# Layer 1 of a convolution-attention hybrid: the norm rows' parts for the experts behind the next image's keys and values

## The chip, the cores and the metric

The kernel runs on one core of one Trainium2 chip, in one launch. The metric is the time of the whole kernel on the device, in microseconds (us). The engines are named as the profile names them: PE is TensorE (matmuls; PEld is its weight load), DVE is VectorE, ACT is ScalarE, POOL is GpSimd, SP is the engine that issues the DMAs here.

## The reference

Eight images of 256 channels and 32 x 32 points pass through two layers. Layer 0 is convolutional attention and a filtered feed-forward network. Layer 1, in which the change lies, treats each image as 1024 tokens of 256 numbers:

```python
t = _to_tokens(x)
t = t + _L1_attn_ref(_ln_t(t), L1_attn_WQ, L1_attn_WK, L1_attn_WV)
t = t + _L1_ffn_ref(_ln_t(t), L1_ffn_Wr, ..., L1_ffn_bo)
x = _from_tokens(t, x)
```

The attention is causal, with one head: scores of queries and keys, the lower triangle kept, exponentials divided by their sum, times the values. The feed-forward part has eight experts of three matrices each, and a gate that is computed from the mean over the images of the second norm's rows:

```python
feat = jnp.mean(x, axis=0)
w = jax.nn.softmax(feat @ Wr + br, axis=-1)
h = jnp.einsum('bfd,edh->bfeh', x, W1) + b1
...
y = jnp.einsum('bfeh,ehd->bfed', h, Wo) + bo
return jnp.einsum('bfed,fe->bfd', y, w)
```

## The kernel before, in words

Layer 0 ends at about 1387 us of the profiled execution, layer 1's attention runs from there to about 1957 us, and the experts from there to the end.

**The attention of layer 1.** One image is one turn of a loop, `together(causal(b), beside(b), 0.85)`. `causal(b)` is the main part: for each of eight blocks of 128 queries, the scores (`s`, two halves of 512 keys), the negated row maximum (`nm`), the exponential (`pr`), mask and sum (`norm`), the turning of the rows (`tp`, copied to `pT`) and, for each pair of blocks, the product with the values (`po`, added to `t`). The stages of a block follow with a lag, so the last products of image b stand among the first scores of image b + 1. `beside(b)` is the work that other images need:

- `first_norm(b + 1)`: the first norm of the next image. The tokens are turned (`tpt`, copied to `zt`), VectorE takes their statistics (`st`, `mv`), GpSimd works out the scale in eight small operations (`y`, `r`), ScalarE scales, TensorE turns back (`tpz`), ScalarE copies to `z`.
- `second_norm(b - 1)`: the same for the image before, into `z2` (the profile calls the turned rows of both norms `z`), after its attention is done. Then `u_d` is stored, the image after next but one is loaded, GpSimd adds the rows to `feat` (line 1583), and `z_parts` splits them.
- `z_parts` (line 1589): the experts multiply in a split precision. For each half of 512 tokens ScalarE writes a rounded upper part, VectorE subtracts it (`parts`) and forms a combination of the two in place (`z`), and two DMAs store the three parts in `z_d`, from where the expert stage fetches them.
- `keys_values_of(b + 1)`: the next image's keys `kk` (four steps `pk` of TensorE, each copied by ScalarE) and values `v` (four steps `pv`, likewise).
- `chore(n)`: n steps of `expert_parts` (line 1500), which splits one expert weight matrix after another (`we`, `parts_w`, four VectorE operations each), until they are used up in image 6.

The scores of image b + 1 need `kk` and `v` of that image, so all of `beside(b)` is emitted before image b + 1 begins. `together` interleaves by estimated times that the generators yield:

```python
for us in main:
    a += us
    while side is not None and s < ratio * a:
        step = next(side, None)
        ...
for _ in side or ():
    pass
```

What is left of the side when the main part ends is emitted without a main step between. The side's estimates are 1.7 for each step of keys or values, 4.8 for each half in `z_parts` and 1.0 for a chore.

**Order on the engines.** Instructions of `pe`, `dve`, `act` and `pool` go through `InOrder`: each is kept behind the instruction that was emitted before it on its engine, so that one that waits holds up all behind it. DMAs on `nc.sync`, and the few instructions that are issued on `nc.vector` or `nc.scalar` directly, may be placed elsewhere by the planner.

**Memory.** PSUM banks for `pk`, `pv`, `po` and half of the norms' turns come from one pool with two buffers (tag `mm`), those for `tp` and the other half of the norms' turns from another with two (tag `tp`), the scores from a third with two. `z2` has one buffer, `parts` two, `we` and `parts_w` one each.

Of the kernel before, what the change touches and what calls it, by code (L numbers as in the profile page):

```python
# [105 lines left out]
def conv_attn_hybrid_kernel(  # L106
# [424 lines left out]
    def keys_values(zb, kk, v, at, wv_s, bank):  # L531
        for h in range(2):
            hs = slice(h * HALF, (h + 1) * HALF)
            for g in range(KC):
                pk = bank([P, HALF], "pk")
                for k in range(KC):
                    pe.matmul(pk, at[:, k, g * P : (g + 1) * P], zb[:, k, hs], start=(k == 0), stop=(k == KC - 1))
                act.copy(kk[:, g, hs], pk)
                yield 1.7
        for j in range(0, NT, 2):  # L540
            pv = bank([P, 2, C], "pv")
            for i in range(2):
                js = slice((j + i) * P, (j + i + 1) * P)
                for k in range(KC):
                    pe.matmul(pv[:, i, :], zb[:, k, js], wv_s[:, k, :], start=(k == 0), stop=(k == KC - 1))
            act.copy(v[:, j : j + 2, :], pv)
            yield 1.7
# [828 lines left out]
    def tokens(stack, early, early_stack):  # L1376
# [55 lines left out]
        def gate(h, room, bank):  # L1432

            nt = NT // 2
            lg = bank([P, nt, NE], "lg")
            for i in range(nt):
                c0 = i * P
                for k in range(KC):
                    pe.matmul(lg[:, i, :], feats[h][:, k, c0 : c0 + P], wrs[:, k, :], start=(k == 0), stop=False)
                pe.matmul(lg[:, i, :], ones[0:1, :], brs, start=False, stop=True)  # L1440
            yield 2.0
            ge = room([P, nt, NE], "ge", 1)
            gs = room([P, nt], "gs", 1)
            dve.tensor_reduce(gs, lg, AX.X, ALU.max)
            dve.tensor_sub(ge, lg, gs.unsqueeze(2).to_broadcast([P, nt, NE]))
            act.activation(ge, ge, AF.Exp)
            yield 1.0
            dve.tensor_reduce(gs, ge, AX.X, ALU.add)
            dve.reciprocal(gs, gs)
            dve.tensor_mul(ge, ge, gs.unsqueeze(2).to_broadcast([P, nt, NE]))  # L1450
            ge4 = room([P, nt, 4, NE], "ge4", 1)
            stacked(ge4, ge, (0, 1, 0, 1))
            yield 1.0
            pwT = bank([4 * NE, HALF], "pwT")
            for i in range(nt):
                pe.transpose(pwT[:, i * P : (i + 1) * P], ge4[:, i].rearrange("p a e -> p (a e)"), ident)
            dve.tensor_copy(wT[:, h * HALF : (h + 1) * HALF], pwT)
            yield 0.5
# [3 lines left out]
        with ExitStack() as l1:  # L1462
# [13 lines left out]
            def load_t(b):  # L1476
                t[b] = early["t"][b % 3] if b % 3 < 2 else two.tile([P, KC, N], F32, tag="t", name="t1", bufs=1)
                nc.sync.dma_start(t[b], t_d[b])
# [59 lines left out]
            zs = {}  # L1538
            chores = expert_parts()

            kk_of, v_of = {}, {}

            def room(shape, tag, bufs):
                return tiny.tile(shape, F32, tag=tag, name=tag, bufs=bufs)
# [9 lines left out]
            def ring(b, name, shape):  # L1554
                return early[name] if b % 2 == 0 else two.tile(shape, F32, tag=name, name=name, bufs=1)

            def first_norm(b):
                z[b] = ring(b, "z", [P, KC, N])
                yield from layer_norm(t[b], z[b], early["zt"], room, bank)

            def keys_values_of(b):
                kk_of[b], v_of[b] = ring(b, "kk", [P, KC, N]), ring(b, "v", [P, NT, C])
                yield from keys_values(z[b], kk_of[b], v_of[b], early["at"], early["wv"], bank_kv)
# [4 lines left out]
            def until(what):  # L1568
                while what not in done:
                    yield 0.7  # L1570

            def second_norm(b):
                yield from until((b, N // QC - 1))
                z2 = two.tile([P, KC, N], F32, tag="z2", name="z2", bufs=1)
                yield from layer_norm(t[b], z2, early["zt"], room, bank)
                nc.sync.dma_start(u_d[b], t[b])
                if b + 3 < B:
                    load_t(b + 3)
                for h, feat in enumerate(feats):
                    half = z2[:, :, h * HALF : (h + 1) * HALF]  # L1580
                    if b == 0:
                        pool.tensor_copy(feat, half)
                    else:
                        pool.tensor_add(feat, feat, half)
                for h in range(2):
                    yield from z_parts(b, h, z2[:, :, h * HALF : (h + 1) * HALF])

            def z_parts(b, h, src):
                parts = two.tile([P, 2, KC, HALF], F32, tag="parts", name="parts")
                act.activation(parts[:, 0].bitcast(F32R), src, AF.Copy, scale=DOWN)  # L1590
                yield 1.2
                dve.tensor_sub(parts[:, 1], src, parts[:, 0])
                yield 1.2
                dve.scalar_tensor_tensor(src, parts[:, 1], -STEP, parts[:, 0], ALU.mult, ALU.add)
                yield 2.4
                nc.sync.dma_start(z_d[b][:, h, :2], parts)
                nc.sync.dma_start(z_d[b][:, h, 2], src)

            def last_norm():

                for qc in range(HALF // QC, N // QC):
                    yield from until((B - 1, qc))
                yield from layer_norm(t[B - 1][:, :, HALF:], z2_last, early["zt"], room, bank)
                dve.tensor_add(feats[1], feats[1], z2_last)
                nc.sync.dma_start(u_d[B - 1][:, :, HALF:], t[B - 1][:, :, HALF:])
                yield 0.5
# [79 lines left out]
            def beside(b):  # L1686

                def chore(n):
                    for _ in range(n):
                        next(chores, None)  # L1690
                        yield 1.0

                if b + 1 < B:
                    yield from first_norm(b + 1)
                yield from chore(3)
                if b >= 1:
                    yield from second_norm(b - 1)
                yield from chore(2)
                if b + 1 < B:
                    yield from keys_values_of(b + 1)  # L1700
                else:
                    yield from last_norm()
                    yield from gate(1, room, bank)
                yield from chore(2)
# [13 lines left out]
            for b in range(B):  # L1718
                together(last() if b == B - 1 else causal(b), beside(b), 0.85)
# [5 lines left out]
        with ExitStack() as l2:  # L1725
# [176 lines left out]
            for n in range(len(pieces) + LAG3):  # L1902
                one_ = two_ = three = iter(())
                if n < len(pieces):
                    v, s = pieces[n]
                    G, h, b = visits[v]
# [34 lines left out]
    with ExitStack() as stack:  # L1941
        tokens(stack, early, early_stack)

    with tc.If(nc.values_load(bad[0:1, 0:1]) > 0):
        layer0_shifted()
        with ExitStack() as stack:
            tokens(stack, None, ExitStack())
# [112 lines left out]
```

## Time and profile before

| | us |
|---|---|
| runs | 3103.87, 3097.66, 3103.89 |
| median | 3103.87 |
| profiled execution | 3097.64 |
| its span | 3095.9 |
| PE busy | 2921.8 (94%) |
| DVE busy | 2340.2 (76%) |
| ACT busy | 1621.0 (52%) |
| POOL busy | 316.6 (10%) |

The span runs from the first to the last instruction of the profiled execution, and the durations in this text are from that execution. The images of the attention begin at 1510.7, 1583.5, 1656.3, 1729.1 and 1802 us (images 2 to 6), the last one at 1876 us.

In the lines of the profile, a row of the timeline has its start in us, the time taken in us, the engine, the line (L73 is the line in `InOrder` by which nearly all instructions are issued, so that they are told apart by their tiles), the operation, output and inputs by the program's names, the shapes, the count of merged instructions, and in brackets the idle time before it and what ended that. A row of the waits has the total in us, how often, and the longest. Tiles with `_e` are the other buffer of the same data (`z` and `z_e`, `kk` and `kk_e`), `te` and `t` are images.

### The profile page before, as it was taken

Reading aid. Unit: us, or ns where it says so; the run is one execution under the profiler, and the core shown is the slowest. Engines: PE = TensorE matmul, PEld = TensorE weight load, DVE = VectorE, ACT = ScalarE, POOL = GpSimd, SP = SyncE. Lnnn points to the kernel's source line nnn. Section 1 sums busy time; section 2 is a strip of 40 time slices with the busy share of each in tenths; the row PEclk is TensorE's granted clock in tenths of the full one; section 3 lists DMA queues with packets and bytes.
Section 4 is the critical chain, followed back from the end, with each engine's and each line's share of the span. In section 5 each row is a group of like instructions: output and inputs, shape, how many; then the busy total and the mean of one; then the engine's idle time right before and its main releaser. Section 6 shows DMA issues by size and latency. Waiting matters only on the chain.

```text
span 3095.9 us, 41592 instructions
## 1 busy us (share of the span) xinstructions
PE 2921.8 (94%) x16802; PEld 1928.7 (62%) x16802; DVE 2340.2 (76%) x2886; ACT 1621.0 (52%) x2440; POOL 316.6 (10%) x453
## 2 busy tenths in 40 slices
PE   6988899989998989889999999999999999999998
PEld 4644555555555555456666666677777777777776
DVE  2378787878787879686666655588988888888887
ACT  2555454545454545434444443565666666666664
POOL 1012111111111110001222222000000000000000
PEclk8999999999999999999999999999999999999999
DMA  6202121121213120103332311421211252112210
GB/s 194 53 5 66 44 60 51 50 60 47 64 38 73 36 61 15 36 23 116 143 131 109 123 65 81 164 72 66 102 68 68 71 201 75 68 68 95 76 68 29
DMA packets 63856, 234.87 MB, mean 76 GB/s; under 512 B 5590, under 2 KB 13862, under 8 KB 54822
## 3 DMA queue, kind: packets, MB, share of 16 engines
q1 hardware_dynamic: 63654, 232.12, 22.8%
q8 instruction: 134, 2.20, 0.3%
q14 instruction: 68, 0.56, 0.1%
HBM read 140.61 MB, written 91.49 MB: 75 GB/s over the span
## 4 chain that ended last, share of the span: by engine, by line
PE 75%; DVE 14%; ACT 6%; POOL 2%; issue 1%; DMA 1%; SPq 0%; ACTq 0%; DVEq 0%; POOLq 0%
PE pm L73 13%; PE pa L73 12%; PE q L73 11%; PE po L73 9%; PE s L73 6%; PE ph L73 6%; DVE o L73 4%; PE pq L73 3%; PE sums L73 3%; DVE x L73 2%; DVE conv L73 2%; PE pz L73 2%; ACT zt_e L73 2%; PE pv L73 2%; PE pp L73 1%
## 5 line engine op out<-in xcount | busy, mean ns | idle before, releaser
L73 PE MATMUL pa<-ze,w 128*128 128x512 f32 x1488 | 423.2, 393 | 0.0
L73 DVE SCALAR_TENSOR_TENSOR x<-hpad,vec,x 128x1024 f32<-128x1024 f32 x248 | 316.8, 1283 | 74.5 <-ACT x L73 67.1
L73 DVE SCALAR_TENSOR_TENSOR conv<-hpad,vec,conv 128x1024 f32<-128x1024 f32 x256 | 327.8, 1284 | 15.2 <-ACT conv L73 9.1
L73 PEld LDWEIGHTS pa<-ze,w 128*128 128x128 f32 x1488 | 278.2, 188 | 63.2 <-issue 3.0
L73 ACT ACTIVATE h<-pa,bn_o,s1a 128x512 f32<-128x512 f32 x256 | 198.6, 776 | 202.2 <-PE pa L73 202.2
L73 ACT ACTIVATE pT<-s 128x1024 f32<-128x1024 f32 x256 | 247.6, 1024 | 89.1 <-PE s L73 89.1
L73 PE MATMUL po<-pT,vT 128*32 128x256 f32 x4096 | 271.0, 382 | 0.0
L73 PE MATMUL q<-h2p,w 128*128 128x512 f32 x768 | 269.0, 459 | 0.0
L73 DVE SCALAR_TENSOR_TENSOR h<-pa,s1b,h 128x512 f32<-128x512 f32 x256 | 191.5, 748 | 95.2 <-PE pa L73 86.2
L73 PE MATMUL ph<-xn,piw 128*128 128x512 f32 x512 | 242.3, 614 | 15.1 <-ACT vpad L73 6.9
L73 PE MATMUL pm<-h,w 128*128 128x512 f32 x512 | 241.0, 593 | 0.0
L73 PE MATMUL q<-z_first,w 128*128 128x512 f32 x768 | 217.0, 391 | 2.8 <-DVE z_first L73 1.7
L73 PE MATMUL pm<-h1p,w 128*128 128x512 f32 x768 | 216.8, 390 | 0.5 <-DVE h1p L73 0.5
L73 PEld LDWEIGHTS q<-h2p,w 128*128 128x128 f32 x768 | 144.6, 188 | 83.1 <-issue 59.6
L73 DVE SCALAR_TENSOR_TENSOR o<-vpad,pe_w,o 128x1024 f32<-128x1024 f32 x128 | 163.7, 1283 | 39.4 <-ACT o L73 36.2
L73 PE MATMUL s<-qst,kst 128*128 128x256 f32 x1024 | 174.0, 313 | 8.5 <-ACT pT L73 5.9
L73 PEld LDWEIGHTS ph<-xn,piw 128*128 128x128 f32 x512 | 93.7, 195 | 130.5 <-issue 99.8
L73 PEld LDWEIGHTS po<-pT,vT 128*32 128x32 f32 x4096 | 120.0, 109 | 83.9 <-PE s L73 2.0
L73 PEld LDWEIGHTS s<-qst,kst 128*128 128x128 f32 x1024 | 138.2, 196 | 45.4 <-issue 29.9
L73 PEld LDWEIGHTS q<-z_first,w 128*128 128x128 f32 x768 | 144.4, 188 | 34.3 <-DVE z_first L73 2.9
L73 PEld LDWEIGHTS pm<-h1p,w 128*128 128x128 f32 x768 | 144.7, 188 | 31.7 <-DVE h1p L73 0.9
L73 PE MATMUL sums<-pT,ones 128*32 128x256 f32 x2048 | 157.4, 379 | 0.0
(281 smaller groups left out, 5108.3 us busy)
## 6 DMA issues: line engine op xcount, KB each, us to landing
ze<-zd SPq DMA_DIRECT2D x29, 1536.0 KB, 6.4
qst<-part SPq DMA_DIRECT2D x32, 512.0 KB, 9.7
kst<-part SPq DMA_DIRECT2D x32, 512.0 KB, 16.3
te<-ud SPq DMA_DIRECT2D x32, 512.0 KB, 4.0
wd<-parts_w SPq DMA_DIRECT2D x20, 768.0 KB, 3.7
w<-wd SPq DMA_DIRECT2D x20, 768.0 KB, 5.8
zd<-parts SPq DMA_DIRECT2D x14, 1024.0 KB, 3.8
ud<-te SPq DMA_DIRECT2D x18, 512.0 KB, 3.4
```

The lines of the kernel that those rows point to most:

```text
L73: return self._tc.keep_in_program_order(method(*args, **kwargs))
```

## The change

`second_norm` no longer runs `z_parts` at its end; it leaves its `z2` in a dictionary, and a new generator `parts_of` takes it from there and runs the same two halves. `beside(b)` calls `parts_of(b - 1)` behind `keys_values_of(b + 1)`; in the last image, where there are no next keys, it calls it ahead of the last norm, behind the two chores that stand between. No instruction is added, removed or given another shape.

```diff
-            kk_of, v_of = {}, {}
+            kk_of, v_of, z2_of = {}, {}, {}
...
                         pool.tensor_copy(feat, half)
                     else:
                         pool.tensor_add(feat, feat, half)
+                z2_of[b] = z2
+
+            def parts_of(b):
+                z2 = z2_of.pop(b)
                 for h in range(2):
                     yield from z_parts(b, h, z2[:, :, h * HALF : (h + 1) * HALF])
...
                 yield from chore(2)
                 if b + 1 < B:
                     yield from keys_values_of(b + 1)
+                    if b >= 1:
+                        yield from parts_of(b - 1)
                 else:
+                    yield from parts_of(b - 1)
                     yield from last_norm()
                     yield from gate(1, room, bank)
                 yield from chore(2)
```

## The prediction

> **What bounds the kernel now.** First the page: TensorE has work for nearly the whole span, VectorE for three quarters. That is an average, so the layer-1 attention, which the diff touches, was read next, image by image (one image of `beside` and `causal` lasts 72.8 us). Of the windows:
>
> ```profile
> core 0: us, PE busy (x) PEld busy (x) DVE busy (x) ACT busy (x) POOL busy (x), PEclk, DMA share, GB/s
> 1583.50:1656.30 72.80, 69.53 (x294) 45.42 (x293) 46.80 (x104) 33.19 (x62) 18.50 (x26) 1.00 0.35 130
> 1656.30:1729.10 72.80, 69.48 (x293) 45.35 (x293) 44.62 (x100) 33.18 (x62) 18.51 (x26) 1.00 0.31 116
> ```
>
> TensorE bounds the stage; VectorE has 28 us free per image. The view of waits, filtered to weight loads in the second window, says what TensorE lacks:
>
> ```profile
> PEld tpz L73 <- ACT zt_e L73: 2.8, 7, 0.8
> PEld pk L73 <- ACT kk L73: 2.7, 1, 2.7
> PEld tpz L73 <- ACT pT L73: 1.1, 1, 1.1
> PEld s L73 <- PE tp L73: 0.8, 1, 0.8
> ```
>
> Two matter. One wait before the keys (pk), and several small ones before the turned rows of a norm (tpz). The timeline from image 4 into image 5 shows what leads to each:
>
> ```profile
> 1705.57 4.68 POOL L73 TENSOR_TENSOR feat<-feat,z 128x1024 f32<-128x1024 f32 x2 [0.62 <-ACT z L73]
> 1708.34 3.00 DVE L73 TENSOR_TENSOR parts<-z,parts 128x1024 f32<-128x1024 f32 x1 [3.33 <-ACT parts L73]
> 1711.26 0.68 DVE L73 TENSOR_TENSOR te<-te,po 128x512 f32<-128x512 f32 x1
> ...
> 1714.74 1.22 DVE L73 TENSOR_REDUCE nm<-s 128x1 f32<-128x1024 f32 x1
> ...
> 1716.06 1.11 ACT L73 ACTIVATE pr<-s,nm 128x1024 f32<-128x1024 f32 x1 [5.32 <-DVE nm L73]
> ...
> 1718.46 3.70 PE L73 MATMUL pk<-z,at 128*128 128x512 f32 x8 [1.83 <-ACT kk L73]
> ...
> 1729.10 0.58 ACT L73 COPY v<-pv 128x512 f32<-128x512 f32 x1 [1.14 <-PE pv L73]
> ...
> 1738.54 0.25 POOL L73 TENSOR_SCALAR y<-mv 128x8 f32<-128x8 f32 x1 [17.29 <-DVE mv L73]
> ...
> 1742.28 3.06 ACT L73 ACTIVATE zt_e<-zt_e,y,r 128x256 f32<-128x256 f32 x6 [1.82 <-POOL y L73]
> ...
> 1742.93 0.27 PEld L73 LDWEIGHTS tpz<-ident,zt_e 128*128 128x128 f32 x2 [0.55 <-ACT zt_e L73]
> ```
>
> (Image 4 begins at 1656.3, image 5 at 1728.9.) The first parts subtraction sits in VectorE's queue ahead of `te<-te,po` and the softmax. It waits 3.33 us for ScalarE, then takes 3.00 instead of its median 1.22. So the last nm comes late, ScalarE sits 5.32 us on it with the kk copies queued behind, and pk stops. In the next image the first norm's chain (statistics, eight small POOL operations, scaling) ends just as TensorE wants tpz: it already waits 0.55. That chain has no slack.
>
> **The change part by part.** Nothing is added or dropped: per image 2 ScalarE copies, 4 VectorE operations and 4 stores move behind the eight kk/v steps. What moves with them is what `together` interleaves. Following its estimates (main counts 48.7 an image, the side may spend 0.85 of that, 41.4), the parts' 9.6 leave the side, so now one weight chore and three of four pk steps fall among the last scores; the fourth pk, all pv and the parts come after the main part has ended, just ahead of the next image's first scores.
>
> *Removed: the pk wait.* Walk TensorE from po at 1705.35, steps from the same timeline (po pair 3.04, half score or pk 1.72, turns 0.54 and 0.66, pv block 6.9). po ends 1708.39, pk 1710.11, turns 1710.65, half score 1712.37. The second pk needs the bank of po, which VectorE frees after `te<-te,po`. Ahead of that now stands the weight chore (four operations, 2.35 us), which starts at 1705.1 and meets POOL's two feat additions. The row first: the parts subtraction, two inputs in the state buffer, took 3.00 and ended 1.1 after POOL. The Trainium skill, SBUF — State Buffer, section "SBUF: two separate sides", says why: VectorE and GpSimd share a port pair as an exclusive lock, held for a whole instruction. By it the chore is shut out as well and ends at 1705.57 + 4.68 + 1.85 = 1712.1, te ends 1712.75, the second pk starts 1712.85 (0.48 lost). By the row of the chore alone (never seen beside feat) it ends 1707.4 and nothing is lost. I take the rule, since the parts row obeys it; it costs 0.4 an image. Then half score 1716.29, pk 1718.01, turns 1718.67, pk 1720.39, pv, and the next image's scores at 1727.3 instead of 1728.9: **1.6 us gained**. ScalarE's nm wait is now covered: the copies TensorE needs (first three kk) stand ahead of the last exponential. Image 1, where feat is two copies of 1.04 us, has no pk wait, and gains 0.3.
>
> *Added: a late norm.* ScalarE reaches the parts only behind the last v copy (1727.5 to 1728.1), so VectorE, idle since about 1722, gets the first subtraction at 1729.1. Spacings of 1.31, 1.14, 1.31 and 1.14 (from the rows of parts) end the four at 1734.0, the second weight chore (2.36) at 1736.3; its data were fetched long before. Only then come the statistics: two pairs 2.15, nm 1.11, two pairs 2.16, ending 1741.75. In the run before they ended at 1738.45 and POOL began at 1738.54. POOL now begins at 1741.8, **3.3 us later** by the clock, 4.9 later against TensorE's own queue. Queued behind on VectorE: the first nm, te and softmax; on ScalarE the first exponential waits for nm, the fourth zt copy stands behind it, and TensorE's turns of the image before wait for that copy's bank. All this lies inside the same 4.9 us. From tpz on, ScalarE, TensorE and VectorE keep their old order, so the shift stays.
>
> *DMAs.* The parts' stores issue 8 to 20 us later on SP. Their reader is the expert stage, hundreds of us later (first stores), and z2 is written again 30 us later; landing takes 3.8. Loads of weights and t are ready-issued on SP and were early. Costed at 0; with that cover gone, at most 4 us at one image.
>
> *Sum.* Images 1 to 2: 3.3 + 1.3 (no stall to win) = 4.6. Three boundaries 2 to 5: 3.3 each, 9.9. Into image 6 no second chore stands there, so 3.3 - 2.36 = +0.9; its small constants were issued at 1393 and the turn of bo waits for nothing. Into image 7 no first norm follows: -1.6. Image 7, where the parts pass only two empty chores: 0. Total **+13.8 us**. Not shown before: how ScalarE, VectorE order falls at image 6 (parts behind or ahead of the norm), -1.6 to +8 there (the upper end if TensorE's two bo turns wait for VectorE); I take +0.9, the nearest row being the other boundaries. The profiled execution took 3097.64 (span 3095.9), so its own time becomes 3111.4. The runs lie in two groups, 3097.7 and 3103.9, median 3103.87; from the median it is 3117.7. I give **3116**, on the median's side.
>
> **The rivals.** *Gain only (faster).* If the first norm's chain has more slack than I read, because statistics slip ahead of the parts, each of five images keeps the pk win: 1.6 to 2.0 each, some -9 us, 3095. For: VectorE's 28 free us, four waits of 4.6 to 5.5 us for weight data that end. Against: VectorE is fed in written order, as the 3.33 us wait ahead of ready softmax work shows, and tpz already waits. It decides at 1.6 us of chain delay: less, and the change wins.
>
> *Cancels.* If parts and chores overlap the pv block more than I think (ScalarE's parts issued in its 1.1 us gaps between v copies), loss and gain meet near 1.6 to 2: within 5 us of 3104. Against: the parts stand behind all v copies.
>
> *Worse.* The late exponential and bank waits add instead of overlapping: another 2 us at five images, or the 8 us at image 6. +22 to +24, about 3127.
>
> *No such change.* That the order is planned back to the old one: the trace of before follows the written order on every compute engine and departs from it only for the bo constants and the DMAs, so under 0.03; it would give 3104.
>
> **How the numbers follow.** About 0.2% (6 us) is what a measurement of this kernel tells from no change. Main case 0.70, worse 0.08: both slower by over 0.2%; a weak tail of the main case, the cancelling rival and no change make same 0.11; gain only, 0.11. The main case spans 3107 to 3124 (rule or row -2, image 6, group of runs). The range drops the lowest and highest tenth: 3098 to 3126.
>
> **What would show it.** Right: no pk wait on kk; VectorE idle 6 to 7 us during pv, then parts subtraction at its 1.22 us and directly ahead of the statistics; POOL's y some 14.5 us after the image's first score instead of 9.6; waits of tp and tpz on ScalarE growing by about 5 us an image; image periods of 76 instead of 72.8, TensorE's busy sum unchanged. Wrong: statistics ahead of the parts, periods of 71, or weight chores ending at 1707.4's place beside feat (the rule).

## The result, and the profile after

The kernel with the change takes 3118.9 us (median of 7 runs, 3110.66 to 3126.01); the kernel before, run beside it, 3103.37 us (7 runs, 3097.66 to 3107.34). The ratio is 1.0052, with a 95% interval of 1.004 to 1.0064: slower by 12 to 20 us. The profiled execution took 3118.9 us, its span is 3117.1.

The span is 21.2 us longer than that of the profile before (3095.9), but not all of that is the change. Three stretches tell it apart, each bounded by the first matmul of a step: up to image 1's first score (1439.5 us before, 1448.4 after), from there to the experts' first matmul (519.5 before, 533.1 after), and the rest (1136.9 before, 1135.6 after). The change lies in the middle one: **+13.6 us**. The 8.9 us of the first stretch have the same matmuls at another clock, as the windows show (ahead of the comma the window and its length, then busy time and instructions of each engine, PEclk, DMA). Before:

```profile
0.00:1439.50 1439.50, 1307.43 (x10306) 775.98 (x10307) 1073.28 (x1162) 697.77 (x1089) 184.46 (x263) 0.96 0.20 56
```

After:

```profile
0.00:1448.40 1448.40, 1323.83 (x10306) 788.18 (x10307) 1073.70 (x1162) 697.83 (x1089) 185.26 (x263) 0.95 0.20 55
```

TensorE's 10306 matmuls took 16.4 us longer, VectorE's and ScalarE's work the same to 0.5 us. No part of the change explains that: the kernel before with nothing left out but the later sums into `feat` (an experiment below) takes 1447.1 us for the same stretch.

In the middle stretch, call "period" the time from an image's first score to that of the next (image 6 is counted from the turn of bo, a small constant, 0.2 us ahead of its first score). For images 1 to 6:

| us | 1 | 2 | 3 | 4 | 5 | 6 |
|---|---|---|---|---|---|---|
| before | 71.1 | 72.8 | 72.7 | 72.8 | 72.8 | 74.3 |
| after | 70.8 | 75.6 | 75.6 | 75.6 | 75.5 | 77.5 |

Image 7, up to the experts, took 83.0 before and 82.6 after. The windows of images 4 and 5, the same view as that shown of before:

```profile
core 0: us, PE busy (x) PEld busy (x) DVE busy (x) ACT busy (x) POOL busy (x), PEclk, DMA share, GB/s
1670.30:1745.90 75.60, 69.70 (x294) 45.32 (x294) 45.95 (x100) 32.97 (x62) 17.62 (x26) 1.00 0.30 112
1745.90:1821.40 75.50, 69.60 (x293) 45.18 (x292) 48.26 (x104) 32.96 (x62) 17.68 (x26) 1.00 0.33 123
```

TensorE is busy as long as before at the same clock (69.5 us an image then); what grew is the time in which it waits. Images 2 and 3 are less clean. Their clock was 0.98, and TensorE's work took about 1.5 us more. Image 2:

```profile
1519.20:1594.80 75.60, 71.32 (x294) 46.14 (x293) 45.94 (x100) 32.96 (x62) 17.64 (x26) 0.98 0.36 133
```

Their periods did not grow, since the slow matmuls fall into time in which TensorE waits in images 4 and 5. In image 2 they are the scores behind tp, which take 4.96 us instead of 3.60, and the wait of 1.64 us for tpz that follows them in image 5 is not there. The waits of weight loads in image 4 (total, how often, longest) name what grew:

```profile
PEld tpz L73 <- ACT zt_e L73: 4.7, 7, 2.5
PEld tp L73 <- ACT zt_e L73: 3.0, 1, 3.0
PEld tpz L73 <- ACT pT L73: 1.1, 1, 1.1
PEld s L73 <- PE tp L73: 0.8, 1, 0.8
...
PEld pk L73 <- DVE te L73: 0.3, 1, 0.3
```

The 2.7 us of pk on ScalarE's kk are gone, 0.3 us on VectorE's te stand there instead. In exchange tpz grew from 2.8 to 4.7, and tp, which had no wait worth a row, has 3.0: together 4.9 us more. The timeline from image 4 into image 5 (image 5's first score at 1745.89) shows both ends:

```profile
1724.00 0.42 DVE L73 TENSOR_SCALAR parts_w<-we 128x512 fp32r<-128x512 f32 x1
1724.44 3.20 PE L73 MATMUL po<-pT,v_e 128*128 128x256 f32 x16
1724.45 0.69 DVE L73 TENSOR_TENSOR parts_w<-we,parts_w 128x512 fp32r<-128x512 f32 x1
1724.66 5.46 POOL L73 TENSOR_TENSOR feat<-feat,z 128x1024 f32<-128x1024 f32 x2 [0.62 <-ACT z L73]
1725.18 2.73 DVE L73 SCALAR_TENSOR_TENSOR parts_w<-parts_w 128x512 fp32r<-128x512 f32 x1
...
1727.94 2.47 DVE L73 TENSOR_SCALAR parts_w<-parts_w 128x512 fp32r<-128x512 f32 x1
...
1730.33 0.67 DVE L73 TENSOR_TENSOR te<-te,po 128x512 f32<-128x512 f32 x1
...
1731.46 1.88 PE L73 MATMUL pk<-z,at 128*128 128x512 f32 x4
...
1745.89 1.88 PE L73 MATMUL s<-kk,z 128*128 128x512 f32 x4
1746.09 0.58 ACT L73 COPY v<-pv 128x512 f32<-128x512 f32 x1 [1.14 <-PE pv L73]
...
1746.57 2.01 ACT L73 ACTIVATE parts<-z 128x1024 fp32r<-128x1024 f32 x2
...
1747.66 1.22 DVE L73 TENSOR_TENSOR parts<-z,parts 128x1024 f32<-128x1024 f32 x1 [7.28 <-ACT parts L73]
...
1754.84 0.42 DVE L73 BATCH_NORM_STATS2 st<-zt_e 128x6 f32<-128x256 f32 x1
...
1760.39 0.25 POOL L73 TENSOR_SCALAR y<-mv 128x8 f32<-128x8 f32 x1 [18.70 <-DVE mv L73]
...
1764.12 3.06 ACT L73 ACTIVATE zt_e<-zt_e,y,r 128x256 f32<-128x256 f32 x6 [3.91 <-POOL y L73]
...
1764.78 0.20 PEld L73 LDWEIGHTS tpz<-ident,zt_e 128*128 128x128 f32 x2 [2.47 <-ACT zt_e L73]
```

The row to see is that of 1747.66: VectorE stood idle for 7.28 us with work behind it, because ScalarE reaches the two parts copies only behind the last v copy at 1746.09. The four parts operations and one weight chore then stand ahead of the first statistics, POOL's y comes 14.5 us after the image's first score (9.6 before), and tpz waits 2.47 us for what it waited 0.55 for.

### The profile page after: what moved, and what is told of

The parts are those of the page before. It is cut to its first block, busy times and chain, and to the rows that moved or that the text cites. A ratio compares the mean times of both kernels' runs of the same rounds, so it can differ in the third digit from the quotient of the medians.

```text
span 3117.1 us, 41600 instructions
## 1 busy us (share of the span) xinstructions
PE 2943.3 (94%) x16802; PEld 1942.2 (62%) x16802; DVE 2343.6 (75%) x2886; ACT 1619.8 (52%) x2440; POOL 311.1 (10%) x453
## 4 chain that ended last, share of the span: by engine, by line
PE 75%; DVE 14%; ACT 5%; POOL 2%; issue 2%; DMA 1%; SPq 0%; ACTq 0%; DVEq 0%; POOLq 0%
PE pm L73 12%; PE pa L73 11%; PE q L73 11%; PE po L73 8%; PE s L73 6%; PE ph L73 6%; DVE o L73 4%; PE pq L73 3%; PE sums L73 3%; DVE x L73 2%; DVE conv L73 2%; PE pz L73 2%; ACT zt_e L73 2%; PE pk L73 2%; PE pv L73 2%
```

## The experiments

Each experiment was timed beside the kernel before, in two groups. Its median was 3102.7 us (45 runs) beside these four: the parts behind the next first norm, the last chore ahead of the parts, ScalarE's share at the old place, and before without the sum into feat. It was 3100.51 (27 runs) beside the other three. Where a total and the periods differ in sharpness, the periods of the profile carry the argument.

**The parts of the image before last, behind the next first norm.** They are placed where the theory of the late norm says that they delay nothing.

```diff
                     yield from first_norm(b + 1)
+                if b >= 2:
+                    yield from parts_of(b - 2)
                 yield from chore(3)
...
                     yield from keys_values_of(b + 1)
-                    if b >= 1:
-                        yield from parts_of(b - 1)
```

> The changed kernel, with the parts moved once more: into the next image's turn, behind its first norm and ahead of the three chores. My theory (the loss is the first norm's statistics standing behind the parts on VectorE, the gain is the pk wait gone, and the two are separate): the pk wait stays gone, POOL's y begins 9.6 us after the image's first score as before, image periods 70.7 (72.8 less 2.1), the whole some 5 x 2.1 = 10 us below before, 3093. Rival (VectorE has no place for 5 us of parts among the first scores wherever they stand): periods of 73 or more, no gain over before.

Measured: 3132.68 us (6 runs), ratio 1.0106 (1.0087 to 1.0124). A clear miss. The part under test did what was expected: y came 9.7 us after the first score, and pk waited for nothing. But the periods of images 2 to 6 were 76.4, 83.9, 76.5, 82.2 and 77.0. The waits of 1580 to 1820 us show a new place:

```profile
PEld tpt L73 <- ACT zt_e L73: 16.9, 3, 7.7
PEld tpz L73 <- ACT zt_e L73: 12.3, 12, 3.2
```

The timeline of image 3 has the cause:

```profile
1633.57 0.43 DVE L73 TENSOR_SCALAR parts_w<-we 128x512 fp32r<-128x512 f32 x1 [3.70 <-DMA wd<-parts_w]
...
1635.83 1.22 DVE L73 TENSOR_REDUCE nm<-s 128x1 f32<-128x1024 f32 x1
...
1637.14 0.79 ACT L73 ACTIVATE pr<-s,nm 128x640 f32<-128x640 f32 x1 [11.08 <-DVE nm L73]
...
1638.46 1.12 PE L73 MATMUL tpt<-ident,t 128*128 128x128 f32 x4 [6.82 <-ACT zt_e L73]
```

`parts_w` has one buffer, so the second of two weight chores in a row waits for the first one's store. Here that wait stands ahead of an nm; ScalarE waits 11.08 us for it with a zt copy queued behind, and TensorE 6.82 us for that copy. Also, the 9.6 us that `parts_of` yields as its estimate moved chores and the second norm later in the interleaving. So the place of the parts moves other waits too, and this run cannot price the late norm alone.

**The same without the estimates.** To take the shift of the interleaving away, the same place with

```diff
-                    yield from parts_of(b - 2)
+                    silent(parts_of(b - 2))
```

where `silent`, a helper that the kernel has, emits without yielding estimated time.

> As e1 (parts behind the next image's first norm), but issued at one go and without their 9.6 of estimates, so that chores and second norm keep the places beside the scores that they have in the changed kernel. The theory of e1's loss: it came from what was displaced (two weight chores close together, the second waiting 3.7 us for its store ahead of a row maximum; the second norm later), not from the parts' own 5 us. Then the waits of tpt on ScalarE (up to 7.7 us) go, and periods are 72 to 73. Rival (5 us of VectorE ahead of a row maximum cost their length): 75 or more in every image.

Measured: 3110.78 us (14 runs), ratio 1.0031 (1.0021 to 1.0042). Half right. The tpt waits are gone, and images 2, 4 and 6 have 71.8, 71.8 and 72.6. Images 3 and 5, in which two weight chores stand in a row, have 79.5 and 80.7:

```profile
1624.34 0.43 DVE L73 TENSOR_SCALAR parts_w<-we 128x512 fp32r<-128x512 f32 x1 [5.41 <-DMA we<-in_wo_dram]
...
1626.60 0.68 DVE L73 TENSOR_TENSOR t<-t,po 128x512 f32<-128x512 f32 x1
...
1628.13 3.78 PE L73 MATMUL s<-kk,z 128*128 128x512 f32 x4 [7.02 <-DVE pr L73]
```

Now the second chore waits 5.41 us for its weight, ahead of `t<-t,po` and a softmax, and TensorE waits 7.02 us. The parts themselves cost about 1.1 us an image there (71.8 against the 70.7 with ScalarE's share early, below); the rest is weight data met at the wrong moment, and a granted clock of 0.96 and 0.94 in images 3 and 5, where the others had 1.00. The waits of the chores on DMA that the prediction saw in the trace of before are free only where VectorE has nothing urgent behind them.

**The last chore ahead of the parts.** One term of the sum moves: the 2.36 us of the weight chore are taken from between parts and statistics and go into the idle time of VectorE.

```diff
                     yield from keys_values_of(b + 1)
+                    yield from chore(2)
                     if b >= 1:
                         yield from parts_of(b - 1)
```

(`chore(2)` at the end of `beside` stays for the last image only.)

> The changed kernel with the two last chore steps of an image moved ahead of the parts, so that the weight chore's four VectorE operations fall into the idle time under the pv matmuls and only the parts stand between image start and statistics. My theory: POOL's y begins 12.1 instead of 14.5 us after the first score, periods of images 2 to 5 73.2 instead of 75.6, image 6 unchanged, in all 4 x 2.4 = 9.5 us below the changed kernel, 3109. Rival (the delay is not VectorE's queue but ScalarE's parts and copies): 75.6 stays.

Measured: 3107.88 us (16 runs), ratio 1.0022 (1.001 to 1.0034). Periods of images 2 to 6: 73.3, 73.3, 73.7, 74.6 and 75.6. y now comes 12.3, 12.3 and 12.6 us after the first score in images 2 to 4, some 2 us earlier than in the changed kernel, and the periods are shorter by as much. Image 4, for one, has its first score at 1659.57:

```profile
1672.19 0.25 POOL L73 TENSOR_SCALAR y<-mv 128x8 f32<-128x8 f32 x1 [16.79 <-DVE mv L73]
```

What delays the statistics delays the image.

**Only ScalarE's share at the old place.** The two upper parts are issued at the end of `second_norm`, where they stood in the kernel before; `parts_of`, behind the values, keeps VectorE's four operations and the stores.

```diff
                 z2_of[b] = z2
+                uppers(b, z2)
+
+            def uppers(b, z2):
+                for h in range(2):
+                    parts = parts_at[b, h] = two.tile([P, 2, KC, HALF], F32, tag="parts", name="parts")
+                    act.activation(parts[:, 0].bitcast(F32R), z2[:, :, h * HALF : (h + 1) * HALF], AF.Copy, scale=DOWN)
...
```

> The changed kernel with ScalarE's two upper parts back at their old place (end of the second norm); only VectorE's four operations and the stores stay behind the keys and values. My theory: VectorE takes the parts in the 7.3 us that it sat idle for ScalarE, the statistics are on time (POOL's y at 9.6 us), the pk wait stays gone, periods 70.7, 3093. Rival (the four VectorE operations are late by their own length): periods above 73, like e2 or worse.

Measured: 3094.53 us (14 runs), ratio 0.9969 (0.9957 to 0.998): faster than both kernels. Periods of images 2 to 6: 70.7 four times, then 72.5. Its timeline, with the next image's first score at 1727.58:

```profile
1708.01 2.02 ACT L73 ACTIVATE parts<-z 128x1024 fp32r<-128x1024 f32 x2
...
1721.99 1.21 DVE L73 TENSOR_TENSOR parts<-z,parts 128x1024 f32<-128x1024 f32 x1
...
1726.49 1.23 DVE L73 SCALAR_TENSOR_TENSOR z<-parts 128x1024 f32<-128x1024 f32 x1
...
1727.58 1.88 PE L73 MATMUL s<-kk,z 128*128 128x512 f32 x4
...
1730.55 0.43 DVE L73 BATCH_NORM_STATS2 st<-zt_e 128x6 f32<-128x256 f32 x1 [0.58 <-ACT zt_e L73]
...
1737.22 0.25 POOL L73 TENSOR_SCALAR y<-mv 128x8 f32<-128x8 f32 x1 [13.04 <-DVE mv L73]
```

The first subtraction starts 5.6 us ahead of the next image's first score instead of 1.8 behind it, the four parts operations fill VectorE's idle time, and y is back at 9.64 us after the first score. The waits of image 4 have lost both, the pk wait and the growth of tpz and tp:

```profile
PEld tpz L73 <- ACT zt_e L73: 2.8, 7, 0.8
...
PEld tpz L73 <- ACT pT L73: 1.1, 1, 1.1
PEld s L73 <- PE tp L73: 0.8, 1, 0.8
```

So the whole loss of the change goes when ScalarE's two copies are put back. VectorE's four operations behind the keys and values cost nothing, as long as they are fed in time.

**Before, without the sum into feat.** What made the subtraction slow, and what that was worth:

```diff
-                        pool.tensor_add(feat, feat, half)
+                        pass
```

The gate's mean then covers the first and the last image alone (VectorE adds the last); TensorE's work is the same.

> The kernel before with GpSimd's feat additions left out (images 1 to 6; the gate's mean is then that of fewer images). My theory of the gain (the pk wait of before came from the first parts subtraction being shut out by the two feat additions): the subtraction takes 1.22 instead of 3.0, the pk wait falls from 1.8 to 0.2 as in image 1 of before, where feat is two short copies, periods 71.0, some 9 us below before, 3094. Rival (the pk wait comes from where the parts stand, whatever GpSimd does): the wait stays at 1.8, no change.

Measured: 3095.51 us (22 runs), ratio 0.9976 (0.9966 to 0.9986). Periods of images 2 to 6: 71.0, 71.1, 71.1, 71.1 and 72.7. The group of the subtraction (shortest, median, longest in ns) has lost its long ones, and the pk wait of image 4 is short:

```profile
L73 DVE TENSOR_TENSOR parts<-z,parts x14: 1205/1219/1226, 1499.5 to 1930.5; 128x1024 f32<-128x1024 f32 x14
```

```profile
PEld pk L73 <- ACT kk L73: 0.9, 1, 0.9
```

Before, the longest was 3.00 us and the wait 2.7. Of the 2.1 us an image that the change can win here, 1.7 are POOL's feat beside the parts, and only the rest is the parts' own place.

**After, without the sum into feat.** The same edit in the changed kernel prices the disputed step of the prediction, the chore held up by feat.

> The changed kernel with GpSimd's feat additions left out (images 1 to 6; the gate's mean is then that of fewer images). It sizes the term that the prediction took from the rule on the shared port: the weight chore beside feat. My theory: the chore's four operations take 0.4 to 0.7 each instead of up to 2.7, but TensorE's wait for po's bank was only 0.25 an image, so periods go from 75.6 to 75.3 and the whole to 1 us below the changed kernel. Rival (the lock's cost is passed on to the late statistics): POOL's y earlier than 14.5 us after the first score, periods 75 or less.

Measured: 3116.9 us (6 runs), ratio to before 1.0047 (1.003 to 1.0065). The last two chore operations take 0.69 and 0.43 us here instead of 2.73 and 2.47, so the hold-up is real. But the periods are 75.6, 75.7, 75.7, 75.7 and 77.4, no shorter than with feat, and TensorE's second pk starts 7.02 us behind po both here and with feat (1724.44, 1731.46):

```profile
1722.36 3.20 PE L73 MATMUL po<-pT,v_e 128*128 128x256 f32 x16
...
1723.10 0.69 DVE L73 SCALAR_TENSOR_TENSOR parts_w<-parts_w 128x512 fp32r<-128x512 f32 x1
...
1723.83 0.43 DVE L73 TENSOR_SCALAR parts_w<-parts_w 128x512 fp32r<-128x512 f32 x1
...
1729.38 1.88 PE L73 MATMUL pk<-z,at 128*128 128x512 f32 x4
```

The hold-up costs nothing here.

**Before, with a delay of the statistics.** The slack of the first norm's chain, measured without any of the change: two operations of the parts' size into a spare buffer, ahead of the statistics.

```diff
             def first_norm(b):
+                if b >= 3:
+                    spare = two.tile([P, 2, KC, HALF], F32, tag="parts", name="parts")
+                    for i in range(2):
+                        dve.tensor_sub(spare[:, i], z[b - 1][:, :, :HALF], z[b - 1][:, :, HALF:])
                 z[b] = ring(b, "z", [P, KC, N])
```

> The kernel before with two idle VectorE subtractions (128x1024, 1.22 us each, into a spare buffer that nothing reads) ahead of the first norm's statistics, in the turns of images 2 to 6; everything else stays. It doses the lateness by itself. My theory (the chain has about 1 us of slack on VectorE and then none): statistics end 1.2 us later, POOL's y 10.8 us after the first score instead of 9.6, periods of images 2 to 5 74.0 instead of 72.8, image 6 unchanged (VectorE idle there), 4.8 us above before, 3108. Rival (VectorE's idle time takes up 2.4 us anywhere): 72.8 stays.

Measured: 3101.87 us (14 runs), ratio 1.0002 (0.999 to 1.0015). The total cannot confirm the few us expected, nor exclude them (+0.15% would be 4.7 us). The profile does: periods of images 2 to 6 were 74.0, 74.4, 74.0, 73.5 and 74.3, where before has 72.8, 72.7, 72.8, 72.8 and 74.3. In image 5, whose first score is at 1736.80:

```profile
1739.37 2.35 DVE L73 TENSOR_TENSOR parts<-z 128x1024 f32<-128x1024 f32 x2
...
1741.64 0.42 DVE L73 BATCH_NORM_STATS2 st<-zt_e 128x6 f32<-128x256 f32 x1
...
1747.19 0.25 POOL L73 TENSOR_SCALAR y<-mv 128x8 f32<-128x8 f32 x1 [18.04 <-DVE mv L73]
```

y comes 10.4 us after the first score instead of 9.6, and 10.8, 11.2 and 10.8 in images 2 to 4. Of 2.35 us, 0.8 to 1.6 reach y, since VectorE was early by the rest. What reaches y is paid to 0.1 us: 1.2, 1.6, 1.2 and 0.8 us of delay lengthen the four periods by 1.2, 1.7, 1.2 and 0.7.

**All of it in one rule.** With y's time after the first score and the period side by side, for images 2 to 5 (left out is image 5 of the kernel with the chore ahead, where the granted clock was 0.98; in images 2 and 3 of the changed kernel the same clock cost nothing, as said above):

| kernel | y after the first score | pk stalled by the parts | period |
|---|---|---|---|
| ScalarE's share early | 9.6 | no | 70.7 |
| before | 9.6 | yes | 72.8 |
| before, with a delay | 10.4 to 11.2 | yes | 73.5 to 74.4 |
| last chore ahead of the parts | 12.3 to 12.6 | no | 73.3 to 73.7 |
| after | 14.5 | no | 75.6 |

Without the stall, the period is 70.7 plus what y is later than 9.6: 70.7 + 4.9 = 75.6. The stall is worth 2.1. The two kernels with the parts behind the first norm are not in the table: their y is on time (9.7), but other waits come on top, so the rule does not hold for them (71.8 and more).

## Why the prediction was right, point by point

**The removed wait: right, and somewhat too small.** The prediction gave 1.6 us an image; the runs show 2.1. Aligned at po (1705.35 before, 1724.44 after, 19.09 apart), the next image's scores began at 1745.89 where before would have had 1728.90 + 19.09 = 1747.99. The mis-sized term is the 0.48 us for the chore shut out by feat. That the chore is shut out was right (Trainium skill, SBUF — State Buffer, section "SBUF: two separate sides": whichever of the two engines is first has the shared ports for its whole instruction): the chore's last two operations took 2.73 and 2.47 us beside feat, and 0.69 and 0.43 without it. (By that section an operation with one input is shut out only in a mode that uses both port pairs. The last one has one input and was shut out; its mode is in no trace here.) But feat is two instructions, and the prediction let all of the chore that was left, 1.85 us, run behind both. In the run the second operation was already under way when feat began and lost nothing, the third ended at 1727.91, soon after the first of feat's two at 1727.36, and only the last, 0.43 us, was left when POOL ended at 1730.12. So te ended at 1731.0, 6.6 us behind po, and the second pk, which starts 7.02 behind po without any hold-up, did not notice. The row of the chore alone would have given the right cost, for the wrong reason.

**The late norm: right to 0.1 us.** Predicted: the first subtraction 1.8 us behind the next image's first score, VectorE idle 6 to 7 us ahead of it, y at 14.5 instead of 9.6. Measured: 1747.66 - 1745.89 = 1.77, 7.28 idle, 14.5. The wait appeared where it was expected, at tpz and tp on ScalarE's zt copies, and totals the 4.9 us. The delay and the moved chore show that it is paid at one for one.

**The sum.** Predicted +13.8, measured +13.6 in the profiled stretch. By images: image 1's period -0.3, as predicted. Images 2 to 5, predicted at 4.9 - 1.6 = 3.3 each, grew by 2.8, 2.9, 2.8 and 2.7: 11.2 instead of 13.2, because more was won at pk. Image 6, predicted at +0.9, has +3.2, and image 7, predicted at 0, -0.4: together 2.8 instead of 0.9. In image 6 y came 11.7 us after the first score (the prediction's steps give 14.5 - 2.36 = 12.1), so the late norm was there as predicted; but the granted clock was another, as the windows of image 6 show. Before, and after:

```profile
1801.70:1876.00 74.30, 69.94 (x296) 45.61 (x295) 38.50 (x89) 33.31 (x62) 18.50 (x26) 1.00 0.14 57
```

```profile
1821.40:1898.90 77.50, 72.84 (x296) 47.32 (x295) 36.35 (x89) 33.28 (x62) 16.84 (x26) 0.96 0.14 55
```

The same 296 matmuls took 2.9 us longer, and here the slow ones lie behind the waits, where nothing hides them; in image 7 TensorE's work took 1.2 less (74.81 before at 0.95, 73.58 after at 0.97). Without the clock the two images together come to 2.8 - 1.7 = 1.1, near the predicted 0.9. The lower clock is probably no accident but a part of the change: without feat it was 0.96 there too, with the chore ahead 0.98, and it follows the waits that the new order makes (figures in the last section). No run varied it by itself. So two misses cancel in the sum, a gain at pk that was 2 us too small in all and a clock that the prediction put at nothing; that the +13.6 agrees better than the terms do is luck.

**The medians** differ by 15.5 us, the interval of the ratio (12 to 20 us) holds 13.6, and the predicted 3116 lies inside the runs of 3110.66 to 3126.01. Here too the clock helps. The seven runs of the changed kernel had granted clocks of 0.968 to 0.977, 0.972 in the mean; the 45 runs of before in the experiments had 0.972 to 0.979, 0.975 in the mean, and among them the time rises by about 1.7 us for each 0.001 of clock lost. By this estimate some 6 of the 15.5 us go with the clock, part of it in stretches that the change does not touch.

**The rivals.** *Gain only* fell: it needed a chain delay of less than 1.6 us, and 4.9 came. The chain does have some slack ahead of y, VectorE's lead of 0.8 to 1.6 us in the kernel with the delay, and none behind it. Yet the kernel with ScalarE's share early is that rival made true, at 2.1 an image. *Cancels* needed parts issued between the v copies; the 7.28 us row shows that they were not. *Worse* fell too: the late exponential lay inside the same 4.9 us, and image 6 had no wait of 8 us. *No such change* fell with the first row of the parts. Stores at 8 to 20 us later cost nothing that can be seen: the experts' stage took 1136.9 us before and 1135.6 after.

**The place of ScalarE's share.** The prediction saw that ScalarE reaches the parts only behind the v copies, and so that VectorE stands idle; it had no price for moving that share alone. The runs give it: a ratio to before of 1.0052 against 0.9969, for two instructions of 1.0 us at another place in ScalarE's queue.

## What to carry to other kernels

Before work is moved into another engine's idle time, look at who feeds that work: it starts when the feeding engine's queue has come to it, and here two copies behind a chain of v copies turned an idle stretch of 7.28 us of VectorE into a delay. Split a moved step by engines, leave the producing part early and move only the part whose engine is short of time. A chain across four engines (statistics, scale, scaling, turn back) whose end is already waited for (0.55 us here) has little slack: VectorE's lead of 0.8 to 1.6 us ahead of the first link, and then each delay is paid in full. And each wait for a DMA in an ordered queue is free only as long as nothing urgent stands behind it.

## What was not expected of the hardware

- VectorE and GpSimd shared the lock by turns: beside feat, VectorE's two operations of 0.69 and 0.43 us took 2.73 and 2.47, and POOL's pair took 5.46 instead of 4.68. The first half took 2.70 and the second 2.81 instead of 2.36 each: the first began 0.48 us before the chore's second operation was done, the second 0.59 before the third was. The wait shows as a longer instruction, not as idle time. The same rows in the kernel with ScalarE's share early, 2.73, 2.47 and 5.47. Which side is served first was not tried by itself.
- The granted clock differs between executions of one kernel by more than small changes are worth: the kernel with the last chore ahead of the parts ran at 3097.0 us at best and at 3117.92 at worst, and among its runs 3103.24 had a clock of 0.977 and 3117.74 one of 0.968. Within one execution it differs as well. In images 2 to 6 it stayed at 1.00 in the kernel before (as it is, without feat and with the delay) and with ScalarE's share early. It left 1.00 in the changed kernel (without feat too, in the same images and at the same places), with the chore ahead of the parts, and in both kernels with the parts behind the first norm. In image 2 of the changed kernel, the 3.4 us up to the end of the wait for tp, and the 3.4 us after:

```profile
1529.10:1532.50 3.40, 0.67 (x7) 0.43 (x6) 3.23 (x12) 0.91 (x3) 0.00 (x0) 1.00 1.04 361
1532.50:1535.90 3.40, 3.40 (x7) 1.84 (x8) 2.46 (x11) 0.89 (x2) 2.02 (x3) 0.50 1.03 357
```

Ahead of the drops in images 3 and 6, TensorE worked 1.13 and 1.31 of 3.40 us. The three drops begin at 1532.5, 1607.6 and 1839.7, which lie 22 and 68 times 3.413 us apart. Counted on in such slots, the emptiest of image 4 (1679.3 to 1682.7) has 1.59 us of work and that of image 5 has 1.94, since the wait falls into two slots, and no drop follows. So in this trace the low clock comes behind the slots with the least work, and whether a wait makes such a slot depends on where it falls. No run tried this by itself. For a change of 0.5% the periods of images at full clock tell more than the totals.
